# Column lists by one subtraction, searches tied to products, and row constants taken beside the single y blocks

## The chip, the cores and the metric

The kernel runs on one core of one Trainium2 chip. The metric is device time in microseconds (us) of one launch. Before the change the median of three runs was 1048.48 us (1046.01 to 1048.81). The hardware profiler also recorded one execution, and every duration below is from that execution.

Engines: TensorE (PE) multiplies matrices, VectorE (DVE) does elementwise work, reductions and searches, ScalarE (ACT) copies, activations and row sums, GpSimd (POOL) index work and indirect DMA (gathers and scatters), and SyncE (SP) issues plain DMA.

## The reference

Two graph layers over 2708 nodes with 1024 features, each with a residual and a layer norm, all in float32. `adj` is a 0/1 matrix with 10979 ones, some four to a row.

```python
# layer 0, attention masked by adj
q = x @ W_q.T + b_q ; k = x @ W_k.T + b_k ; v = x @ W_v.T + b_v
z = (q @ k.T) / sqrt(1024) * adj
z = where(z == 0, -10000, z)
x = layernorm(x + relu(softmax(z, axis=1) @ v))
# layer 1
x = layernorm(x + adj @ (x @ weight) + bias)
```

## The kernel before

**Sparse form.** The kernel lists the non-zero columns of each row of `adj` and gathers only those rows of `x`. If a list does not fit, or a product of exactly zero makes the mask ambiguous, a flag sends the program to a dense version; with these inputs the sparse one alone runs.

**Lists (`list_columns`, L235 to L252).** `adj` is read in 22 blocks of 128 rows (the last has 20), each cut into six column ranges of growing width, with eight ones stored behind each range. Per range one DVE search (`max_index`, L242) returns the positions of the first eight ones, in order. The ones behind the range stand for "no more". L244 marks the positions that lie inside the range, L247 adds the range's start, L248 sets the others to zero, and three `max` with two `match_replace` keep the 24 largest numbers as the row's `keys`. `count_columns` (L254) sums the row on ACT and then loads a later block of `adj` into the same one of three buffers.

**Families and records.** `sort_begin(f)` and `sort_end(f)` (L657, L678) sort the rows of a family by number of neighbours (family 0: blocks 0 to 7; family 1: blocks 8 to 21). `records_out` scatters one record of 28 words per row (24 columns, then row, degree, offset, one unused word) to DRAM, in sorted order, and reads all back as `tabs`. From then on a block means 128 rows of like degree, with as many gather slots as `SLOTS` says. The 32 longest rows are cut into pieces, the "hub", by `deal_hub`, a generator that is continued by each `next(deal)`.

**Stages, in order of time.**

1. M = W_q^T W_k is formed in 28 half products of four matmuls (`product_of_m`, L757). `EARLY` says how many lists are emitted among them.
2. y = x M for family 0 in four pairs of blocks (`y_pair`), seven half products each, by a scheme that saves one product in eight. Lists, counts and sorting are hung between half products in the table `between`. In a pair, DVE adds one half into another, and the last product needs the bank that such an add has read.
3. y for blocks 8 to 21 one at a time (`y_block`, L386): 16 matmuls each, results copied by ACT. `firsts` holds every fourth matmul.
4. Pair steps: attention sums are turned and multiplied by W_v in ten pairs (`project_pair`), with one step "mean" for the rows that have no neighbours.
5. Layer 1 in the same form, over gathered rows of `x1`, which layer 0 has scattered.

**Attention on DVE.** Beside stages 3 and 4 DVE scores each gathered row against y (L1027, L1143) and sums the rows by their weights (L1086, L1162). A planner hands out these jobs: each step adds the time that DVE is thought to have (`credit`), a job takes its estimated cost from it (1.5 us, and 2.6 us per slot), and jobs that a coming pair needs are forced. A job's first score follows the product before the last.

**Row constants (`row_constants`, L1281).** The test for exact zeros needs x.u per row, u being one vector. In the last three pair steps POOL gathers x for 23 blocks of sorted rows (22 and the hub), 9, 9 and 5 at a time, and DVE multiplies each by u and adds up (L1286). u is spread over the partitions into `u_bc`, which is the tile `part`, once the hub has done with it (L1418). `test_scores` (L1297) uses the sums in layer 1.

**Order.** The program order and the dependencies are the author's; a scheduler orders each engine's instructions ahead of time, by readiness in its own estimate, with program order as priority. On the chip each engine takes its instructions in that order. `follow(later, earlier)` adds a dependency, which moves an instruction behind a matmul in this order. `high_priority` puts the adds of products first among what is ready.

Of the kernel before, what the change touches and what calls it, by code (L numbers as in the profile page):

```python
# [9 lines left out]
F32 = mybir.dt.float32  # L10
BF16 = mybir.dt.bfloat16
I32 = mybir.dt.int32
# [26 lines left out]
KEYS = 24  # L39
RANGES = 6  # L40
CLASSES = list(range(1, 14)) + [15, 17, 20, 24]
EARLY = 13
G1 = 9
RB = 5
REC = 28
ROW, DEG, OFF = 24, 25, 26

# [36 lines left out]
def sparse_part(ctx, tc, x, xT, adj, wqT, wkT, wvT, bq, bk, bv, w1, b1, out):  # L84
# [28 lines left out]
    with es:  # L113
# [12 lines left out]

        def load_rows(dst, src, r0, n, queue=nc.sync):
            m = n // 16 * 16
            queue.dma_start(out=dst[:m], in_=src[r0:r0 + m])
            if m < n:  # L130
                queue.dma_start(out=dst[m:n], in_=src[r0 + m:r0 + n])

# [73 lines left out]

        cuts = [round(N * (i / RANGES) ** 2) for i in range(RANGES + 1)]
        loaded, sorted_, products, applied, began, between = [], [], [], [], [], {}

        AW = N + 8 * RANGES  # L210
        ends = lists.tile([P, RANGES, 8], F32, name="ends")
        base = lists.tile([P, RANGES, 8], F32, name="base")
        for i in range(RANGES):
            nc.vector.memset(ends[:, i], float(cuts[i + 1] - cuts[i]))
            nc.vector.memset(base[:, i], float(cuts[i] + 1))

# [17 lines left out]

        def list_columns():  # L235
            b = listed[0]
            listed[0] += 1
            n, a = rows[b], loaded[b]

            at = lists.tile([P, RANGES, 8], U16, name="at_a", bufs=2)  # L240
            for i in range(RANGES):
                nc.vector.max_index(at[:n, i], ones[:n, :8], a[:n, cuts[i] + 8 * i:cuts[i + 1] + 8 * i + 8])  # L242
            there = lists.tile([P, RANGES, 8], F32, name="there", bufs=2)
            nc.vector.tensor_tensor(there[:n], at[:n], ends[:n], op=ALU.is_lt)  # L244
            few = lists.tile([P, 8 * RANGES], F32, name="few", bufs=2)
            few3 = few.rearrange("p (i k) -> p i k", k=8)
            nc.vector.tensor_tensor(few3[:n], at[:n], base[:n], op=ALU.add)  # L247
            nc.vector.tensor_tensor(few3[:n], few3[:n], there[:n], op=ALU.mult)  # L248
# [132 lines left out]
        def y_store(b, yo):  # L381
            r0, n = b * P, rows[b]
            o0 = r0 - FAMILY * P * (b >= FAMILY)
            nc.sync.dma_start(out=y_ds[b >= FAMILY][o0:o0 + n, :D], in_=yo[:n])

        def y_block(b):  # L386
            yo = yos[b % 3]
            to = halves_of(yo)
            firsts = []
# [12 lines left out]
            load_x()  # L402
            y_store(b, yo)
# [353 lines left out]
        def product_of_m(acc, a, w, start, stop):  # L757
# [477 lines left out]

        STEP, Y_END, Y_LATE, PAIR, EVICT, FLIP, END, SLOT, SMALL = 14.2, 4.8, 1.8, 24.3, 7.5, 2.2, 3.3, 2.6, 1.5
        got, xb_bc, xb_pools, pair_x = {}, [], [], {}
# [38 lines left out]
        nc.vector.memset(c_rows, 0.0)  # L1276
        c_left = list(range(NB + 1))

        u_bc = part

        def row_constants(count):  # L1281
            for k in [c_left.pop(0) for _ in range(count)]:
                n = P if k in (0, NB) else rows[k]
                at = rec_h[:, ROW:ROW + 1] if k == NB else tab0[:, ROW:ROW + 1] if k == 0 else tabs[:n, k, ROW:ROW + 1]
                xg = gather_at(x, at, n, g_tile(), behind=products[-2])
                nc.vector.scalar_tensor_tensor(junkv[:n], xg[:n], 1.0, u_bc[:n], op0=ALU.mult, op1=ALU.mult,  # L1286
                                               accum_out=c_rows[:n, k:k + 1])

# [8 lines left out]
        def test_scores():  # L1297
# [58 lines left out]
        for i, (kind, b) in enumerate(steps):  # L1356
# [29 lines left out]
            if kind == "y":  # L1386
                if FAMILY + 1 <= b < FAMILY + 5:
                    next(deal)
                if 6 <= b - FAMILY < 11:
                    k0 = 3 * (b - FAMILY - 6)  # L1390
                    records_out(*later_records, k0, min(k0 + 3, NB - FAMILY), products[-2])
                if b == FAMILY + 11:
                    records_back(1)
                    nc.sync.dma_start(out=bias_bc, in_=bv.to_broadcast([P, D]))
# [16 lines left out]
            else:  # L1411
# [20 lines left out]
        for p in pending:  # L1432
            p[0](*p[1:])
        assert not jobs and not c_left

# [431 lines left out]
```

## Time and profile before

| | |
|---|---|
| median of three runs | 1048.48 us |
| the profiled execution's own time | 1040.17 us |
| its span, first to last instruction | 1038.3 us |
| mean granted PE clock | 0.977 |
| PE, DVE, POOL, ACT busy | 962.3, 824.4, 564.5, 459.0 us |
| moved by DMA | 229.24 MB, mean 221 GB/s |

Stages by the timeline: M until 132 us, y pairs until 248, single y blocks until 431, pair steps until about 735, layer 1 to the end. A group of instructions is shown by line, engine, operation, tiles, shapes and count; then its busy time and the mean of one, and the idle time ahead of it with what ended that idle time. A line of the waits says which instruction of an engine waited for which of another: us in total, number of times, longest. In the timeline, the square brackets hold the idle time before an instruction.

### The profile page before, as it was taken

To read this page: it belongs to the slowest core of one execution; us is meant where nothing else is said; L and a number is where in the kernel's file an instruction comes from. 1 tells how busy PE (TensorE), PEld (TensorE's weight loads), DVE (VectorE), ACT (ScalarE), POOL (GpSimd) and SP (SyncE) were. 2 spreads that over 40 slices of the span, in tenths; PEclk is the share of its full clock that TensorE was granted. 3 is DMA by queue.
4 is the path that set the end of the run, shared out by engine and by line. 5 is a ranking of instruction groups with operands and counts; after the bars stand their busy time and mean duration, and the time that the engine had idled before them with its cause. 6 is when DMAs were issued, how large, how long until landed. Compare 5 with 4: busy or idle time off the path is not lost.

```text
span 1038.3 us, 10579 instructions
## 1 busy us (share of the span) xinstructions
PE 962.3 (93%) x2723; PEld 453.5 (44%) x2723; DVE 824.4 (79%) x1851; ACT 459.0 (44%) x1142; POOL 564.5 (54%) x455
## 2 busy tenths in 40 slices
PE   7979996899999999999999899997899999988994
PEld 6434443444444444455544444443444444434441
DVE  8999998982768987998999798976569886868532
ACT  4634473554534354224745453334323444361832
POOL 3841045231567656245466576572578888768420
PEclk9989998999999999999999899998999999989998
DMA  9465786666889777257448777698597699987741
GB/s 348 148 189 176 222 275 198 214 203 216 216 249 318 254 216 225 97 145 216 165 124 239 241 222 236 227 282 308 167 308 226 218 297 314 312 249 196 219 109 44
DMA packets 103070, 229.24 MB, mean 221 GB/s; under 512 B 19678, under 2 KB 47078, under 8 KB 103000
## 3 DMA queue, kind: packets, MB, share of 16 engines
q0 software_dynamic: 51152, 159.06, 50.1%
q1 hardware_dynamic: 51848, 69.41, 20.6%
q8 instruction: 23, 0.38, 0.1%
q14 instruction: 47, 0.39, 0.1%
HBM read 218.09 MB, written 33.64 MB: 242 GB/s over the span
## 4 chain that ended last, share of the span: by engine, by line
PE 40%; DVE 25%; DMA 13%; issue 10%; ACT 6%; POOL 5%; SPq 1%; POOLq 0%; DVEq 0%; ACTq 0%
PE po L313 22%; PE po L393 11%; DVE at_a L242 6%; PE tr L393 5%; DMA g<-in_x_dram,tabs 4%; DVE r L1463 2%; DMA xr<-x_d,tabs 2%; ACT junks L989 2%; POOL g L485 2%; DMA g<-x_d,tab 1%; DVE t L335 1%; DVE r L1086 1%; PE tr L942 1%; DMA wq_i<-in_wqT_dram 1%; ACT t L1003 1%
## 5 line engine op out<-in xcount | busy, mean ns | idle before, releaser
L313 PE MATMUL po<-t,s_all 128*128 128x512 f32 x320 | 145.2, 595 | 8.5 <-DVE xr L335 3.1
L485 POOL DMA_INDIRECT g<-in_x_dram,tabs x84 | 111.6, 1329 | 69.5 <-ACT r L1084 14.0
L393 PE MATMUL po<-m,xt 128*128 128x512 f32 x288 | 124.7, 592 | 0.1
L1463 DVE SCALAR_TENSOR_TENSOR r<-g,valid,r 128x1024 f32<-128x1024 f32 x77 | 98.1, 1280 | 16.3 <-issue 6.7
L313 PEld LDWEIGHTS po<-t,s_all 128*128 128x128 f32 x320 | 59.8, 190 | 87.4 <-issue 73.1
L989 ACT ACTIVATE junks<-t,lnm 128x1024 uint8<-128x1024 f32 (+1 forms) x40 | 45.8, 1144 | 115.5 <-DVE lnm L987 115.1
L1027 DVE SCALAR_TENSOR_TENSOR junkv<-yg,g 128x1024 uint8<-128x1024 f32 x69 | 84.3, 1222 | 10.1 <-DMA g<-in_x_dram,tabs 5.5
L485 POOL DMA_INDIRECT g<-x_d,tabs x66 | 77.1, 1168 | 23.2 <-issue 17.6
L1086 DVE SCALAR_TENSOR_TENSOR r<-g,pr,r 128x1024 f32<-128x1024 f32 x64 | 82.0, 1281 | 6.4 <-ACT r L1084 5.8
L393 PEld LDWEIGHTS po<-m,xt 128*128 128x128 f32 x288 | 54.6, 190 | 68.2 <-issue 67.4
L242 DVE FIND_INDEX8 at_a<-ones,a 128x8 uint16<-128x83 f32 (+3 forms) x132 | 82.0, 627 | 0.0
L313 PE MATMUL po<-wv,s_all 128*128 128x512 f32 x160 | 75.1, 611 | 6.8 <-DVE t L335 6.8
L943 ACT COPY rT<-tr 128x512 f32<-128x512 f32 x76 | 41.5, 588 | 84.0 <-PE tr L942 70.2
L313 PE MATMUL po<-w,rT 128*128 128x512 f32 x160 | 73.7, 601 | 4.5 <-DVE t L1500 4.2
L258 ACT ACTIVATE junk<-a 128x2756 uint8<-128x2756 uint32 (+1 forms) x22 | 55.0, 2501 | 49.5 <-issue 31.5
L313 PE MATMUL po<-t,rT 128*128 128x512 f32 x160 | 74.3, 607 | 0.9 <-DVE t L335 0.4
L464 ACT ACTIVATE junka<-xt 128x128 f32<-128x128 f32 x168 | 51.8, 308 | 50.1 <-PE po L313 16.7
L313 PE MATMUL po<-wv,rT 128*128 128x512 f32 x160 | 73.2, 606 | 0.0
L313 PE MATMUL po<-w,s_all 128*128 128x512 f32 x160 | 72.5, 593 | 0.0
L1027 DVE SCALAR_TENSOR_TENSOR junkv<-xr,g 128x1024 uint8<-128x1024 f32 x37 | 45.4, 1226 | 18.9 <-DMA g<-in_x_dram,tabs 11.0
L393 PE MATMUL tr<-m,xt 128*128 128x512 f32 x128 | 55.6, 592 | 0.0
L1473 ACT COPY xr<-bias 128x1024 f32<-128x1024 f32 (+1 forms) x22 | 22.8, 1043 | 68.3 <-DVE t L1500 49.7
(418 smaller groups left out, 1868.4 us busy)
## 6 DMA issues: line engine op xcount, KB each, us to landing
xt<-in_xT_dram SPq DMA_DIRECT2D x21, 512.0 KB
y_d<-yo SPq DMA_DIRECT2D x21, 512.0 KB
a<-in_adj_dram SPq DMA_DIRECT2D x21, 413.5 KB
a<-in_adj_dram SPq DMA_DIRECT2D x21, 338.5 KB
a<-in_adj_dram SPq DMA_DIRECT2D x21, 263.5 KB
wq_i<-in_wqT_dram SPq DMA_DIRECT2D x8, 512.0 KB
wk_i<-in_wkT_dram SPq DMA_DIRECT2D x8, 512.0 KB
wv<-in_wvT_dram SPq DMA_DIRECT2D x16, 256.0 KB
```

Source lines behind the costliest of these rows:

```text
L242: nc.vector.max_index(at[:n, i], ones[:n, :8], a[:n, cuts[i] + 8 * i:cuts[i + 1] + 8 * i + 8])
L258: put = nc.scalar.activation(junk[:n], loaded[b][:n, :AW].bitcast(U32), AF.Sign, accum_out=cnt[:n, b:b + 1])
L313: put = nc.tensor.matmul(acc, a[:, k], w[:, k], start=start and k == 0, stop=stop and k == DC // 2 - 1, skip_group_check=True)
L393: put = nc.tensor.matmul(po, xts[b][:, c, :], m_q[c // 4][h][:, c % 4], start=(c == 0), stop=(c == DC - 1))
L464: put = nc.scalar.activation(junka[:, :xt.shape[2]], xt[:, c, :], AF.Copy, accum_out=xs[:, c, b:b + 1])
L485: nc.gpsimd.indirect_dma_start(out=dst[:n], out_offset=None, in_=src, in_offset=bass.IndirectOffsetOnAxis(ap=at, axis=0), bounds_check=N - ...
L943: nc.scalar.copy(rT[:, g * 4:g * 4 + 4, :], tr)
L989: nc.scalar.activation(junks[:n], t[:n], AF.Square, bias=nm[:n], accum_out=vs[:n])
L1027: put = nc.vector.scalar_tensor_tensor(junkv[:n], yg[:n], scale, xg[:n], op0=ALU.mult, op1=ALU.mult, accum_out=s)
L1086: nc.vector.scalar_tensor_tensor(r[:n], xg[j][:n], pr[:n, j:j + 1], r[:n], op0=ALU.mult, op1=ALU.add)
L1463: put = nc.vector.scalar_tensor_tensor(r[:n], xg[:n], ok[:n, j:j + 1], r[:n], op0=ALU.mult, op1=ALU.add)
L1473: follow(nc.scalar.copy(xr[:n], bias1[:n]), last_norm, same=True)
```

## The change

Five things change together.

- **Lists.** The threshold tile `ends` now holds the range's width plus i/16, and one subtraction, `ends - at`, takes the place of compare, add and multiply. A found column gives a number of at least 1, whose fraction tells the range; a missing one gives less than 1. `max` and `match_replace` work on these numbers, so a row's list comes in another order. `sort_begin` turns them into column numbers with six further DVE operations per family, on 128x192 and 128x336 elements. The cuts follow a formula for that (75 i² + i + 2) and move by up to three columns.
- **Searches tied to products.** The first search of a list now follows a matmul: the half product just made in stage 1, the one it hangs on in stage 2.
- **Other places.** `EARLY` is 12, not 13; the y pairs take 2, 3, 3 and 2 lists, not 3, 3, 3 and 0; `sort_begin(1)` comes after the last y pair, not after the third.
- **Row constants of family 1** come from plain rows of x: beside the single y blocks 9 to 13, three blocks at a time, SP loads 128 rows into `part`, DVE multiplies by u. Load and product each follow a matmul of that y block. The sums go into the unused word of the records.
- **Row constants of family 0 and the hub** are gathered as before, but beside single y blocks 10 to 14 and 16 (2, 2, 2, 1, 1 and 1). `u_bc` has a tile of its own, in the place of `bias_bc`, which is loaded later. The planner takes 3.9 us of credit at five steps. The scores of blocks with one slot come one pair step earlier.

```diff
+END2, END1, END0 = 75, 1, 2
-EARLY = 13
+EARLY = 12
-ROW, DEG, OFF = 24, 25, 26
+ROW, DEG, OFF, CON = 24, 25, 26, 27
...
-        cuts = [round(N * (i / RANGES) ** 2) for i in range(RANGES + 1)]
+        cuts = [0] + [END2 * i * i + END1 * i + END0 for i in range(1, RANGES + 1)]
...
-            nc.vector.memset(ends[:, i], float(cuts[i + 1] - cuts[i]))
-            nc.vector.memset(base[:, i], float(cuts[i] + 1))
+            nc.vector.memset(ends[:, i], cuts[i + 1] - cuts[i] + i / 16)
...
-        def list_columns():
+        def list_columns(behind=None):
...
-                nc.vector.max_index(at[:n, i], ones[:n, :8], a[:n, cuts[i] + 8 * i:cuts[i + 1] + 8 * i + 8])
-            there = lists.tile([P, RANGES, 8], F32, name="there", bufs=2)
-            nc.vector.tensor_tensor(there[:n], at[:n], ends[:n], op=ALU.is_lt)
+                put = nc.vector.max_index(at[:n, i], ones[:n, :8], a[:n, cuts[i] + 8 * i:cuts[i + 1] + 8 * i + 8])
+                if i == 0 and behind is not None:
+                    follow(put, behind)
             few = lists.tile([P, 8 * RANGES], F32, name="few", bufs=2)
-            few3 = few.rearrange("p (i k) -> p i k", k=8)
-            nc.vector.tensor_tensor(few3[:n], at[:n], base[:n], op=ALU.add)
-            nc.vector.tensor_tensor(few3[:n], few3[:n], there[:n], op=ALU.mult)
+            nc.vector.tensor_tensor(few.rearrange("p (i k) -> p i k", k=8)[:n], ends[:n], at[:n], op=ALU.subtract)
...
         def sort_begin(f):
...
+            ks = keys[:, bs, :]
             got = lists.tile([P, nb, KEYS], F32, name=f"got{f}")
-            nc.vector.tensor_scalar(got, keys[:, bs, :], 0.0, None, op0=ALU.is_gt)
+            back = lists.tile([P, nb, KEYS], I32, name=f"back{f}")
+            nc.vector.tensor_copy(back, ks)
+            past_end = lists.tile([P, nb, KEYS], F32, name=f"past_end{f}")
+            nc.vector.tensor_sub(past_end, ks, back)
+            nc.vector.tensor_scalar(got, past_end, 256.0 * END2, 32.0 * END2 + 16.0 * END1, op0=ALU.mult, op1=ALU.add)
+            nc.vector.tensor_mul(past_end, past_end, got)
+            nc.vector.scalar_tensor_tensor(past_end, past_end, END2 + END1 + END0 + 1.0, back, op0=ALU.add, op1=ALU.subtract)
+            nc.vector.tensor_scalar(got, ks, 1.0, None, op0=ALU.is_ge)
+            nc.vector.tensor_mul(ks, past_end, got)
...
             while done < EARLY * worked // (7 * DC // 2):
-                list_columns()
+                list_columns(put)
...
-            for k in range(min(3, NB - done)):
+            for k in range(min((2, 3, 3, 2)[b // 2], NB - done)):
                 if k:
-                    between[first + 2 * k] = [lambda put: list_columns()]
+                    between[first + 2 * k] = [list_columns]
                 else:
-                    list_columns()
+                    list_columns(began[-1])
...
                 records_back(0)
+            if b == 6:
                 sort_begin(1)
...
-        bias_bc = hp.tile([P, D], F32, name="bias_bc", tag="bias")
+        u_bc = hp.tile([P, D], F32, name="u_bc", tag="bias")
...
+        def constants_of(xg, n, to, behind):
+            put = nc.vector.scalar_tensor_tensor(junkv[:n], xg[:n], 1.0, u_bc[:n], op0=ALU.mult, op1=ALU.mult,
+                                                 accum_out=to)
+            if behind is not None:
+                follow(put, behind)
+
+        def plain_constants(firsts):
+            for k in range(3):
+                if c_plain:
+                    b = c_plain.pop(0)
+                    n = rows[b]
+                    load_rows(part, x, b * P, n, behind=firsts[k])
+                    constants_of(part, n, c_nat[:n, b - FAMILY:b - FAMILY + 1], firsts[k + 1])
...
+            nc.vector.tensor_copy(c_rows[:, FAMILY:NB], tabs[:, FAMILY:, CON].bitcast(F32))
...
+                if b == FAMILY + 1:
+                    bcast_rows(u_bc, u_col)
+                if 2 <= b - FAMILY < 7 or b == FAMILY + 8:
+                    row_constants((2, 2, 2, 1, 1, 0, 1)[b - FAMILY - 2])
+                if b == FAMILY + 6:
+                    rec1 = later_records[2]
+                    nc.vector.tensor_copy(rec1[:, :, CON:].bitcast(F32), c_nat.unsqueeze(2))
...
                 (y_last if b == NB - 1 else y_block)(b)
+                if 1 <= b - FAMILY < 6:
+                    plain_constants(y_firsts)
+                    credit -= 3 * DOT
...
-                if i == len(steps) - 4:
-                    bcast_rows(u_bc, u_col)
-                if i >= len(steps) - 3:
-                    row_constants((9, 9, 5)[i - len(steps) + 3])
-                if i == len(steps) - 2:
+                if i == len(steps) - 3:
                     for b_ in single:
                         single_scores(b_)
```

More of the change, by code (lines that the diff above doesn't have):

```diff
@@ L125, in sparse_part, with load_rows @@
         wb = tc.alloc_tile_pool(name="wb", bufs=1)
-        def load_rows(dst, src, r0, n, queue=nc.sync):
+        def load_rows(dst, src, r0, n, queue=nc.sync, behind=None):
             m = n // 16 * 16
-            queue.dma_start(out=dst[:m], in_=src[r0:r0 + m])
+            puts = [queue.dma_start(out=dst[:m], in_=src[r0:r0 + m])]
             if m < n:
-                queue.dma_start(out=dst[m:n], in_=src[r0 + m:r0 + n])
+                puts.append(queue.dma_start(out=dst[m:n], in_=src[r0 + m:r0 + n]))
+            if behind is not None:
+                for put in puts:
+                    follow(put, behind)
         bq_sb = const.tile([P, DC], F32, name="bq_sb")
@@ L205, in sparse_part @@
         nc.vector.memset(keys, 0.0)
-        cuts = [round(N * (i / RANGES) ** 2) for i in range(RANGES + 1)]
+        cuts = [0] + [END2 * i * i + END1 * i + END0 for i in range(1, RANGES + 1)]
+        assert cuts[-1] == N
         loaded, sorted_, products, applied, began, between = [], [], [], [], [], {}
@@ L211, in sparse_part @@
         ends = lists.tile([P, RANGES, 8], F32, name="ends")
-        base = lists.tile([P, RANGES, 8], F32, name="base")
         for i in range(RANGES):
-            nc.vector.memset(ends[:, i], float(cuts[i + 1] - cuts[i]))
-            nc.vector.memset(base[:, i], float(cuts[i] + 1))
+            nc.vector.memset(ends[:, i], cuts[i + 1] - cuts[i] + i / 16)
         a_bufs = [la.tile([P, AW + 4], F32, name=f"a{k}", bufs=1) for k in range(3)]
@@ L384, in y_store @@
             nc.sync.dma_start(out=y_ds[b >= FAMILY][o0:o0 + n, :D], in_=yo[:n])
+        y_firsts = []
         def y_block(b):
@@ L388, in y_block @@
             to = halves_of(yo)
-            firsts = []
+            firsts = y_firsts
+            firsts.clear()
             for h in range(NH):
@@ L1233, in finish_pair @@
                 scatter(x1_d[:, :], b, P, t, "x1")
-        STEP, Y_END, Y_LATE, PAIR, EVICT, FLIP, END, SLOT, SMALL = 14.2, 4.8, 1.8, 24.3, 7.5, 2.2, 3.3, 2.6, 1.5
+        STEP, Y_END, Y_LATE, PAIR, EVICT, FLIP, END, SLOT, SMALL, DOT = 14.2, 4.8, 1.8, 24.3, 7.5, 2.2, 3.3, 2.6, 1.5, 1.3
         got, xb_bc, xb_pools, pair_x = {}, [], [], {}
@@ L1276, in sparse_part @@
         nc.vector.memset(c_rows, 0.0)
-        c_left = list(range(NB + 1))
-        u_bc = part
+        c_nat = xa.tile([P, NB - FAMILY], F32, name="c_nat", bufs=1)
+        nc.vector.memset(c_nat, 0.0)
+        c_plain, c_left = list(range(FAMILY, NB)), list(range(FAMILY)) + [NB]
+        def constants_of(xg, n, to, behind):
+            put = nc.vector.scalar_tensor_tensor(junkv[:n], xg[:n], 1.0, u_bc[:n], op0=ALU.mult, op1=ALU.mult,
+                                                 accum_out=to)
+            if behind is not None:
+                follow(put, behind)
+        def plain_constants(firsts):
[5 more added lines that the diff above has]
+                    constants_of(part, n, c_nat[:n, b - FAMILY:b - FAMILY + 1], firsts[k + 1])
         def row_constants(count):
@@ L1285, in row_constants @@
                 xg = gather_at(x, at, n, g_tile(), behind=products[-2])
-                nc.vector.scalar_tensor_tensor(junkv[:n], xg[:n], 1.0, u_bc[:n], op0=ALU.mult, op1=ALU.mult,
-                                               accum_out=c_rows[:n, k:k + 1])
+                constants_of(xg, n, c_rows[:n, k:k + 1], products[-1])
         def single_scores(b):
@@ L1393, in sparse_part @@
                     records_back(1)
+                    bias_bc = hp.tile([P, D], F32, name="bias_bc", tag="bias")
                     nc.sync.dma_start(out=bias_bc, in_=bv.to_broadcast([P, D]))
                 (y_last if b == NB - 1 else y_block)(b)
+                if 1 <= b - FAMILY < 6:
+                    plain_constants(y_firsts)
+                    credit -= 3 * DOT
                 if 3 <= b - FAMILY < 7:
@@ L1433, in sparse_part @@
             p[0](*p[1:])
-        assert not jobs and not c_left
+        assert not jobs and not c_left and not c_plain
         xb_pool.release()
```

## The prediction

> **What bounds the kernel now.** First the page's busy times, then the engines by stage, to see who limits where.
>
> ```profile
> PE 962.3 (93%) x2723; PEld 453.5 (44%) x2723; DVE 824.4 (79%) x1851; ACT 459.0 (44%) x1142; POOL 564.5 (54%) x455
> ```
>
> ```profile
> 26.00:132.00 106.00, 99.50 (x238) 44.37 (x237) 104.89 (x349) 48.93 (x58) 41.78 (x31) 0.97 0.60 185
> 132.00:248.00 116.00, 101.97 (x248) 45.92 (x247) 94.86 (x348) 60.57 (x168) 43.35 (x39) 0.96 0.70 224
> 248.00:431.00 183.00, 182.92 (x483) 81.21 (x482) 140.04 (x235) 77.86 (x296) 103.97 (x78) 1.00 0.75 225
> 431.00:640.00 209.00, 199.02 (x654) 98.41 (x653) 189.66 (x371) 96.93 (x230) 125.90 (x92) 0.98 0.66 198
> 640.00:735.00 95.00, 86.36 (x219) 38.79 (x217) 73.70 (x149) 39.16 (x93) 45.03 (x39) 0.96 0.76 255
> ```
>
> The columns after start, end and length are PE, weight loads, DVE, ACT and POOL, then clock, DMA share and GB/s. PE is the long engine: the end comes sooner only where PE stands still. In the single y blocks (248 to 431) it never does. While M is formed DVE is busy 104.89 of 106 us. So I ask next what PE waited for, first up to 250 us, then from 400 to 735.
>
> ```profile
> PE po L313 <- DVE at_a L242: 10.7, 1, 10.7
> PE tr L313 <- DVE m L335: 6.5, 1, 6.5
> PE po L313 <- DVE yo L335: 3.3, 2, 2.7
> ...
> PE po L313 <- DVE t L335: 9.3, 5, 5.3
> PE tr L942 <- DVE r L1086: 5.0, 3, 4.1
> PE mm L1180 <- DVE tops L1177: 2.4, 1, 2.4
> PE po L313 <- DVE nms L1056: 1.5, 1, 1.5
> ```
>
> Early, 20.5 us, all for DVE. The timeline of PE shows the three longest places:
>
> ```profile
> 57.23 6.17 PE L313 MATMUL tr<-wk_o,wq_o 128*128 128x512 f32 x8 [6.50 <-DVE m L335]
> ...
> 164.07 5.66 PE L313 MATMUL po<-y_t,xt 128*128 128x512 f32 x8 [10.74 <-DVE at_a L242]
> ...
> 715.78 6.28 PE L313 MATMUL po<-wv,s_all 128*128 128x512 f32 x8 [5.31 <-DVE t L335]
> 721.90 3.60 PE L313 MATMUL po<-t,s_all 128*128 128x512 f32 x8
> ```
>
> Eight matmuls take 3.60 us, but 6.17, 5.66 and 6.28 right after these waits: 7.3 us more. DVE's timeline tells why it was late. At 57 us the add that frees the bank stood behind the searches of three lists (35.8 to 56.5); at 164 us the add started at 163.34, behind searches too. At 715 us the add stood behind row-constant products, and those behind gathers that took up to 11 us in the chain that ended last.
>
> ```profile
> L1286 DVE SCALAR_TENSOR_TENSOR junkv<-g,part 128x1024 uint8<-128x1024 f32 x22 | 26.8, 1217 | 4.4 <-DMA g<-in_x_dram,tabs 4.1
> L248 DVE TENSOR_TENSOR few<-few,there 128x48 f32<-128x48 f32 x21 | 9.4, 447 | 0.2
> L247 DVE TENSOR_TENSOR few<-at_a,base 128x48 f32<-128x48 uint16 x21 | 8.4, 402 | 0.0
> L244 DVE TENSOR_TENSOR there<-at_a,ends 128x48 f32<-128x48 uint16 x21 | 7.3, 347 | 0.2
> ```
>
> **What the Trainium skill says.** "TensorE: Matmul & The Clock Gate", Part 1: PE's clock halves after an idle window of some 3.4 us and returns after as long a busy one. The trace agrees: 2.6, 2.1 and 2.7 us lost behind idle times of 6.50, 10.74 and 5.31 us. "SBUF — State Buffer", Who interferes with whom: a DVE instruction with two SBUF inputs waits while GpSimd reads SBUF. The trace agrees: L244 has a median of 208 ns but up to 1270, at 40 to 58 and 130 to 149 us, where POOL adds. "DMA: Bandwidth & Descriptors", Issuing engines are not separate DMA queues: SP's and POOL's transfers share the 16 engines, so moved loads compete with gathers; no single line here shows it, though the DMA share reached 0.97 in 312 to 338 us.
>
> **The change part by part.**
>
> *Lists.* Two of three small operations go. Records overlap by 0.08 us, so a list loses (347 - 80) + (447 - 80) = 0.63 us of DVE, 22 lists 13.9 us. At least 22 x 2 x 0.13 = 5.7, if the remaining subtraction meets all the POOL waits. I take 0.5 a list, 11 us.
>
> *Decoding.* Six more operations per family. Like forms took 241 to 348 ns on 128x192 and 315 to 485 ns on 128x336 (L661, L702, L703): 6 x 0.30 + 6 x 0.40 - 12 x 0.08 = 3.2 us.
>
> *Fewer lists early.* A list is 6 searches at 3.66 us, then 0.11 for the subtraction and 0.7 for max and replace, 4.5 us. Up to the end of the first y pair 14 are due instead of 16. DVE loses there 2 x (4.5 + 0.5) + 14 x 0.5 - 1.3 = 15.7 us. It was saturated and made PE wait 17.2 us by then.
>
> *Ties.* A search can no longer be put ahead of an add whose product ends first. A tied search holds what is behind it on DVE (adds, keys, sorting, the hub), and PE waits for the adds. M needs 28 x 3.43 = 96 us of PE; DVE now has 12 x 4.5 = 54 for lists, 7.3 for adds, 12.4 for differences, 6.3 for sorting and some 4 for POOL's locks, 84 us. It fits, tightly. Of 20.5 + 4.6 (clock) = 25.1 us I take back 20; the bounds are 10 and 25.
>
> *Last y pair.* Two lists (9 us), the rest of the hub's search (some 9), decoding and sorting (9) and adds (2) want 29 of its 24 us, so the sort ends some 5 us late. It was covered by 19 us of idle DVE in 234 to 260. PE can go to the next y block meanwhile; late next are the records, not due before y block 14. I count 1 us, bounds 0 and 8.
>
> *Constants.* The last three pair steps lose 23 gathers (POOL 1.11 us each) and 23 products (1.22 us each, 28 us of DVE). PE's waits from 640 on are 5.31 + 1.47 + 0.44 + 0.43 + 0.37 = 8.0, with the clock 10.7 us. I take 9; bounds 3 and 11.
>
> What moves lands beside the single y blocks. DVE has 183 - 140 = 43 us idle there. The planner's arithmetic, done by hand with 3.9 us taken at five steps, pushes one piece of block 0 (five scores, five sums, 12.6 us) from y block 20 into the step "mean", where two pieces are then forced. Left are 43 - 28 + 12.6 = 27.6 us. `part` is one buffer: load, product, load. The products follow the loads' matmuls by a quarter block, 13.73 / 4 = 3.43 us. A load of that size landed 5.1 us after its issue (x's at 196.85, used at 202.35), so each holds DVE 1.7 us: 14 x 1.7 = 24 us, just inside. PE asks nothing of DVE there: ACT copies the results.
>
> SP is held too, with x's next block and y's store behind; x has four buffers, three blocks (41 us) ahead. DMA: the hardware queue moved 69.41 MB in 20.6% of the span, 1.6 us per 512 KB, the software queue 1.7. 14 loads and 9 gathers are 38 us more; 25% of 183 is 46 us free. POOL's 9 gathers (10 us) queue ahead of x's gathers; POOL idled 79 of 183 us. The transposes for `u_bc` cost PE 1.04 us either way. `bias_bc` comes after y block 19 has begun and is used at 441 us, so its load is hidden. `records_out` now waits for the constants on POOL, with gathers behind: one y block of slack.
>
> *Pair steps.* 12.6 us more DVE work before pair (0, 7), whose last sum was done at 477 us and turned on PE at 505. DVE idled 19 us in 431 to 640, so most is absorbed. I count 5 us of PE, bounds 0 and 13.
>
> Sum: -20 + 1 - 9 + 5 = -23 us. The span goes from 1038.3 to 1015, the profiled execution's own time from 1040.17 to 1017. The median stood 8.3 us above that, so 1025 (1048.48 - 23).
>
> **The rivals.**
>
> *Given back (1038).* Early waits shrink by 15 only, the pair steps return 12: -15 + 1 - 9 + 12 = -11. For it: DVE saturated at 431 to 572. Against: 27 us between block 0's end and its use.
>
> *Ties bind (1036).* Searches wait for products while DVE has nothing else; half the early gain goes: -10 + 1 - 9 + 6 = -12. For it: 84 of 96 us leaves little to idle. Against: DVE ran behind PE throughout.
>
> *Slower (1064): the single `part` buffer.* If a load lands late and DVE stands for it in order, each of 14 holds DVE not 1.7 but 5.1 us: 71 us, 44 beyond the cover. DVE is saturated at the pair steps, so PE pays it: -20 - 9 + 1 + 44 = +16. It decides from where 14 h - 27.6 exceeds the other 28, h = 4.0 us. For it: gathers took up to 11 us under load. Against: at y blocks 9 to 13 the planner gives few jobs, so a held DVE delays little.
>
> *It doesn't do what it says.* A longer first range could overfill a list and send rows to the flag. Counting the ones of the inputs by the new cuts, 19 rows overfill where 20 did, all among the first 23: they are hub rows. Under 1 in 100.
>
> **How the numbers follow.** Forecast 0.48 (1014 to 1036: -20 becoming -25 or -12, +5 becoming 0 or +8); given back 0.20; ties bind 0.10; slower 0.16; all cancelling within the bound, or unforeseen, 0.06. Telling from no change takes about 0.3%, 1045 to 1052. The first three make faster 0.78; the rest leave 0.05 for same and 0.17 for slower. The range 1009 to 1051 leaves out most of the slower case and little at the bottom. The likeliest's own range is 1014 to 1036.
>
> **What would show it.** Lists right: L244 and L248 gone, some 11 to 17 us of DVE busy with them. Ties right: PE's waits up to the last y pair under 8 us, and M ending at 123 us, not 132. Constants right: no L1286 after 640, no wait over 2 us in the last three steps. Wrong: DVE waiting on DMA into `part` for over 30 us, PE waits in 431 to 640 (by the old clock) above 20 us, or PE waiting for the sort's matmul behind the last y pair.

## The result, and the profile after

The kernel became slower: a median of 1090.39 us (1087.77 to 1094.22) against 1047.24 us of the kernel before on the same chip, a ratio of 1.0423 with an interval of 1.0374 to 1.0473. The profiled execution took 1089.38 us, its span 1087.6 us, 49.3 more than the span before. A ratio, here and below, is taken from the executions that count as fast (within 1.5% of the fastest of the same kernel); one of the four of e5 does not and enters only its median.

Lines have moved: L242, L335, L1027, L1086 and L1286 before are L245, L336, L1041, L1100 and L1296 after. First the page's busy times of the changed kernel.

```profile
PE 969.2 (89%) x2723; PEld 458.4 (42%) x2723; DVE 810.2 (74%) x1816; ACT 464.0 (43%) x1142; POOL 552.6 (51%) x441
```

DVE lost 14.2 us of work, as the lists promised, and its share fell from 79 to 74%. The time did not follow. The stretches by stage of the changed kernel (after start, end and length: PE, weight loads, DVE, ACT, POOL, clock, DMA share, GB/s) show where it went wrong.

```profile
26.00:128.40 102.40, 97.83 (x234) 43.46 (x233) 90.06 (x300) 46.47 (x56) 48.53 (x35) 0.98 0.62 190
128.40:244.70 116.30, 103.57 (x248) 46.49 (x247) 96.48 (x364) 62.70 (x170) 35.55 (x35) 0.96 0.67 211
244.70:442.40 197.70, 185.02 (x490) 82.10 (x488) 120.09 (x223) 69.30 (x264) 91.97 (x70) 0.97 0.76 234
442.40:476.60 34.20, 0.01 (x1) 0.01 (x1) 31.45 (x45) 8.54 (x30) 14.74 (x13) 0.57 0.52 174
...
676.00:780.00 104.00, 103.58 (x266) 47.44 (x265) 65.25 (x137) 48.87 (x116) 32.74 (x26) 1.00 0.56 177
```

M and the y pairs end at 244.7 us, 3.3 sooner. The end of layer 0 (676 to 780) is clean: PE is busy for 103.58 of 104 us. But between 442.4 and 476.6 PE does nothing at all. The timeline of PE names the places, with the three longest waits in brackets.

```profile
187.34 5.62 PE L314 MATMUL po<-y_t,xt 128*128 128x512 f32 x8 [8.25 <-DVE yo L336]
...
403.21 5.15 PE L448 MATMUL po<-m,x_last 128*32 128x256 f32 x64 [12.32 <-ACT yo L334]
...
476.60 0.48 PE L1184 MATMUL tr<-ident,nm 128*128 128x128 f32 x1 [34.56 <-DVE nm L1163]
```

The last line is the hub's first turning, the step that follows the y blocks; it came at 430.90 before. In four pieces, by the spans:

| up to | before | after | difference |
|---|---|---|---|
| end of the y pairs | 248.0 | 244.7 | -3.3 |
| the hub's first turning | +182.9 | +231.9 | +49.0 |
| layer 1's first turning (742.65 and 784.90) | +311.75 | +308.3 | -3.4 |
| the end | +295.65 | +302.7 | +7.0 |

The whole loss lies beside the single y blocks. There DVE's own waits tell it, first of the kernel before (248 to 430.9), then of the changed one (244.7 to 476.6).

```profile
DVE junkv L1027 <- DMA g<-in_x_dram,tabs: 11.0, 7, 2.3
DVE alike L616 <- PE tr L615: 9.9, 1, 9.9
DVE junkv L1027 <- PE tr L393: 7.4, 1, 7.4
DVE r L1086 <- ACT r L1084: 5.8, 4, 1.6
```

```profile
DVE junkv L1296 <- DMA part<-in_x_dram: 40.7, 11, 6.4
DVE junkv L1041 <- DMA g<-in_x_dram,tabs: 19.4, 6, 6.5
DVE alike L620 <- PE tr L619: 9.9, 1, 9.9
```

The two stretches as a whole, before and after (columns as above):

```profile
248.00:430.90 182.90, 182.82 (x482) 81.11 (x481) 139.94 (x235) 77.75 (x296) 103.97 (x78) 1.00 0.75 225
...
244.70:476.60 231.90, 185.02 (x491) 82.11 (x489) 151.55 (x267) 77.84 (x293) 106.71 (x83) 0.91 0.72 226
```

So 49.0 us of length are 11.6 us more work of DVE and 37.4 us more idle time, and 40.7 us of idle time are one wait, for the loads into `part`. DVE's timeline shows the round:

```profile
322.36 1.23 DVE L1296 SCALAR_TENSOR_TENSOR junkv<-part,u_bc 128x1024 uint8<-128x1024 f32 x1 [2.79 <-DMA part<-in_x_dram]
...
327.71 1.23 DVE L1296 SCALAR_TENSOR_TENSOR junkv<-part,u_bc 128x1024 uint8<-128x1024 f32 x1 [4.11 <-DMA part<-in_x_dram]
```

One product of 1.23 us, and the next 5.35 us later; the rest is standing: a load starts when the product before has freed `part`, and DVE stands for it. From 312 to 352 us DVE was busy for 13.3 of 40 us, all of it row constants. The scores of the next piece came at 352.28, behind the last of these.

How did that reach PE, whose results ACT copies? By ACT's queue:

```profile
361.31 0.30 ACT L1079 ACTIVATE pr<-scores,nms 128x6 f32<-128x6 f32 x1 [21.41 <-DVE nms L1070]
...
381.99 0.30 ACT L1079 ACTIVATE pr<-scores,nm 128x4 f32<-128x4 f32 x1 [12.96 <-DVE nm L1070]
...
393.28 1.05 ACT L484 COPY yg<-y_bc 128x1024 f32<-128x1024 f32 x1 [8.85 <-DVE junkv L1041]
...
402.59 0.57 ACT L334 COPY yo<-po 128x512 f32<-128x512 f32 x1
```

The softmax's exponential (L1079) waits for DVE's maximum, a copy into a tile of gathered y (L484) for DVE's last reading of that tile, and the copies of y stand behind both. At 390.9 PE had no free bank until the copy at 402.59: 12.3 us. The rest of DVE's lag came due at the hub: PE waited 34.6 us, and DVE was busy for 31.45 of the 34.2 us from 442.4 to 476.6.

### The profile page after: what moved, and what is told of

It reads as the page before. It is cut to its first block, busy times and chain, and to the rows that moved or that the text cites. A ratio compares the mean times of both kernels' runs of the same rounds, so it can differ in the third digit from the quotient of the medians.

```text
span 1087.6 us, 10470 instructions
## 1 busy us (share of the span) xinstructions
PE 969.2 (89%) x2723; PEld 458.4 (42%) x2723; DVE 810.2 (74%) x1816; ACT 464.0 (43%) x1142; POOL 552.6 (51%) x441
## 3 DMA queue, kind: packets, MB, share of 16 engines
q0 software_dynamic: 49232, 152.14, 45.9%
## 4 chain that ended last, share of the span: by engine, by line
PE 44%; DVE 19%; DMA 12%; issue 12%; POOL 8%; ACT 3%; SPq 0%; POOLq 0%; DVEq 0%; ACTq 0%
PE po L314 27%; PE po L397 8%; PE tr L397 4%; PE tr L314 3%; POOL g L489 3%; DMA xr<-x_d,tabs 3%; DVE r L1100 2%; DVE junkv L1041 2%; DMA g<-x_d,tabs 2%; DVE at_a L245 2%; POOL tab_d L724 2%; DVE t L336 1%; DVE r L1498 1%; POOL wk_i L304 1%; DMA g<-x_d,tab 1%
## 5 line engine op out<-in xcount | busy, mean ns | idle before, releaser
L489 POOL DMA_INDIRECT g<-in_x_dram,tabs x84 | 115.7, 1378 | 90.9 <-DVE got L670 28.7
L1041 DVE SCALAR_TENSOR_TENSOR junkv<-yg,g 128x1024 uint8<-128x1024 f32 x84 | 102.3, 1218 | 31.8 <-DMA g<-in_x_dram,tabs 20.5
L1498 DVE SCALAR_TENSOR_TENSOR r<-g,valid,r 128x1024 f32<-128x1024 f32 x77 | 97.9, 1280 | 11.6 <-DMA g<-x_d,tabs 9.0
L1100 DVE SCALAR_TENSOR_TENSOR r<-g,pr,r 128x1024 f32<-128x1024 f32 x64 | 81.8, 1280 | 3.4 <-ACT r L1098 2.9
L245 DVE FIND_INDEX8 at_a<-ones,a 128x8 uint16<-128x234 f32 (+5 forms) x132 | 82.2, 627 | 0.0
L314 PE MATMUL po<-wv,s_all 128*128 128x512 f32 x160 | 72.5, 593 | 3.0 <-DVE s_all L1215 1.6
L943 POOL DMA_INDIRECT x_d<-t,tabs x22 | 27.1, 1233 | 65.0 <-ACT rstd L1014 25.9
L473 POOL DMA_INDIRECT xr<-in_x_dram,tabs x22 | 26.9, 1221 | 53.9 <-DVE scores L1050 33.3
## 6 DMA issues: line engine op xcount, KB each, us to landing
wk_i<-in_wkT_dram SPq DMA_DIRECT2D x8, 512.0 KB, 10.9
```

Source lines behind the costliest of these rows:

```text
L245: put = nc.vector.max_index(at[:n, i], ones[:n, :8], a[:n, cuts[i] + 8 * i:cuts[i + 1] + 8 * i + 8])
L314: put = nc.tensor.matmul(acc, a[:, k], w[:, k], start=start and k == 0, stop=stop and k == DC // 2 - 1, skip_group_check=True)
L489: nc.gpsimd.indirect_dma_start(out=dst[:n], out_offset=None, in_=src, in_offset=bass.IndirectOffsetOnAxis(ap=at, axis=0), bounds_check=N - ...
L943: put = nc.gpsimd.indirect_dma_start(out=dst, out_offset=bass.IndirectOffsetOnAxis(ap=tabs[:n, b, ROW:ROW + 1], axis=0), in_=src[:n], in_o ...
L1041: put = nc.vector.scalar_tensor_tensor(junkv[:n], yg[:n], scale, xg[:n], op0=ALU.mult, op1=ALU.mult, accum_out=s)
L1100: nc.vector.scalar_tensor_tensor(r[:n], xg[j][:n], pr[:n, j:j + 1], r[:n], op0=ALU.mult, op1=ALU.add)
```

## The experiments

All ratios are to the kernel before, run in turn with each; the medians take in more executions, so a ratio is not always the quotient of the two. The runs were on four chips (e1 to e4; e5 to e8; e9 to e11; e12), so runs of different groups are compared by their ratios.

| | kernel | median, us | before, us | ratio | interval |
|---|---|---|---|---|---|
| e1 | lists, ties and places | 1039.51 | 1043.64 | 0.9963 | 0.9933 to 0.9994 |
| e2 | constants alone | 1094.55 | 1043.64 | 1.0508 | 1.0438 to 1.0579 |
| e3 | whole change, no plain loads | 1042.41 | 1043.64 | 0.9994 | 0.9973 to 1.0015 |
| e4 | whole change, nine buffers | 1060.43 | 1043.64 | 1.0166 | 1.0097 to 1.0235 |
| e5 | e1, degrees read later | 1035.53 | 1043.89 | 0.9841 | 0.9766 to 0.9915 |
| e6 | e1 untied | 1030.69 | 1043.89 | 0.9853 | 0.9786 to 0.9921 |
| e7 | e3 without the credit | 1072.36 | 1043.89 | 1.0249 | 1.0184 to 1.0313 |
| e8 | e5, nine constants moved | 1041.67 | 1043.89 | 0.9979 | 0.9960 to 0.9998 |
| e9 | e5 untied | 1033.58 | 1045.50 | 0.9882 | 0.9847 to 0.9917 |
| e10 | e8 untied, softmax tied | 1042.77 | 1045.50 | 0.9982 | 0.9965 to 0.9998 |
| e11 | e9, softmax tied | 1032.32 | 1045.50 | 0.9862 | 0.9823 to 0.9902 |
| e12 | one subtraction alone | 1033.18 | 1043.70 | 0.9890 | 0.9855 to 0.9926 |

**Which half, and what of it (e1 to e4).** e1 is the changed kernel with the row constants put back:

```diff
-                if 1 <= b - FAMILY < 6:
-                    plain_constants(y_firsts)
-                    credit -= 3 * DOT
...
+                if i >= len(steps) - 3:
+                    row_constants((9, 9, 5)[i - len(steps) + 3])
```

> Lists, ties and their places as in the changed kernel; row constants as before (all 23 gathered in the last three pair steps). Theory A (the loss comes from VectorE standing on the plain loads of x) and theory B (it comes from the work moved beside the single y blocks) both give the early part alone: the y pairs ended 3.3 us sooner in the changed kernel, so 1044, at most 2 us away. Theory C (lists that arrive late or in another order slow the sort, the records and the attention behind them) gives over 1060, with PE waits in the pair steps that look like those of the changed kernel.

e2 is the other half on the kernel before (EARLY 13, `list_columns` as before, with `plain_constants`).

> The kernel before with the new row constants alone: plain rows of x beside single y blocks 9 to 13, gathers beside 10 to 14 and 16, credit of 3.9 us at five steps; lists and their places as before. Theories A and B: the whole loss, 1047 + 46 = about 1093, with DVE waits on the loads into part of some 40 us and one PE wait of over 25 us behind the last y block. Theory C: under 1060.

e3 takes the loads out of the changed kernel and leaves the products in place; they multiply u by itself, so the constants of family 1 are left out:

```diff
-                    load_rows(part, x, b * P, n, behind=firsts[k])
-                    constants_of(part, n, c_nat[:n, b - FAMILY:b - FAMILY + 1], firsts[k + 1])
+                    constants_of(u_bc, n, c_nat[:n, b - FAMILY:b - FAMILY + 1], firsts[k + 1])
```

> The changed kernel without the 14 plain loads of x: the 14 products stay in their places, tied to the same matmuls, but multiply u by itself, so the constants of family 1 are not computed. Theory A: the 40.7 us of DVE waits on the loads go, and with them PE's 12.3 and 34.6 us; 1090 - 47 = 1043, perhaps 5 less as the later stalls go too. Theory B (the moved products and the pushed piece are too much work): at most the 11 us of PE's wait for the copies, so over 1075.

e4 keeps the loads and gives each another buffer:

```diff
-                    load_rows(part, x, b * P, n, behind=firsts[k])
-                    constants_of(part, n, c_nat[:n, b - FAMILY:b - FAMILY + 1], firsts[k + 1])
+                    xg = g_tile()
+                    load_rows(xg, x, b * P, n, behind=firsts[k])
+                    constants_of(xg, n, c_nat[:n, b - FAMILY:b - FAMILY + 1], firsts[k + 1])
```

> The changed kernel with the plain rows loaded into the nine rotating buffers of the gathers instead of the one tile part; loads and products keep their ties, a quarter block apart. Theory A with the single buffer as the cause: a load no longer waits for the product before, so a hold is at most a landing of 4.0 to 5.1 less 3.43, under 1.7 us each, 24 us in all instead of 41; DVE's lag falls by 17 us or more and the PE wait of 34.6 us by as much: 1065 to 1073. If the tie of a product a quarter block behind its load were the cause, it stays over 1080. Theory B: over 1080 as well, but with no DVE wait on the loads.

Theory A stands, rivals B and C fall; only e4 came out 5 us below the range that was expected of it. The constants alone cost 5.1% and carry the same wait at the hub (35.7 us), with 32.5 us of DVE waits on the loads; the lists alone cost nothing (0.996). Without the loads, with every product still in its place, the whole 4.2% goes, and PE's wait at the hub falls from 34.6 to 1.9 us. With nine buffers 2.6 of the 4.2% come back. DVE's waits of e4 from 245 us on:

```profile
DVE junkv L1296 <- DMA g<-in_x_dram,tabs: 12.3, 3, 6.3
DVE junkv L1296 <- DMA g<-in_x_dram: 11.5, 4, 5.7
```

The second line is what is left of the 40.7 us. The first is new: DVE now stands for three of the gathered constants. Why those came late was not tried. PE's wait at the hub was 14.5 us. One rival is left open in the remaining 1.7%: the loads are also traffic beside the gathers. DVE's waits for gathered rows at the scores (L1041) were 19.4 us in the changed kernel, against 11.0 before. In e4, with the same loads, they were 6.4, which speaks against it; but no run moves the same bytes with no product behind them.

**What remained without the loads (e7, e8, e10).** e3 was no faster than before, though its end of layer 0 was as clean. I blamed the piece of block 0 that the planner's charge pushes behind the y blocks, and took the charge out:

```diff
-        STEP, ..., SMALL, DOT = 14.2, 4.8, 1.8, 24.3, 7.5, 2.2, 3.3, 2.6, 1.5, 1.3
+        STEP, ..., SMALL, DOT = 14.2, 4.8, 1.8, 24.3, 7.5, 2.2, 3.3, 2.6, 1.5, 0.0
```

> The changed kernel without the 14 plain loads (the products multiply u by itself, so family 1's constants are not computed) and with no credit taken by the planner for them. Without the loads alone it took as long as before although the early part and the end of layer 0 had gained some 12 us. Theory P (the piece of block 0 that the planner pushed from the y blocks into the step of the mean makes the new waits of 16 us between 430 and 630 us): 8 to 12 us less than without the loads, about 1032. Theory W (the 28 us of products on VectorE make it late wherever the pieces are placed): within 4 us of 1042.

A miss, and in the other direction: by the ratios some 27 us slower than e3. Two of PE's waits in e7:

```profile
PE tr L956 <- DVE tops L1186: 13.8, 1, 13.8
...
PE po L448 <- ACT yo L334: 9.1, 1, 9.1
```

With the piece back beside the y blocks, DVE is late for the hub even with no load to stand for. The charge was not the harm; it was what kept DVE's lag from being larger. Theory P falls, and theory W falls with it in its number. That a piece of 12.6 us is worth 27 us is more than either theory had, and why was not tried. With the piece pushed, the products did find some room, as e3's stretch of the y blocks shows:

```profile
244.70:431.40 186.70, 184.84 (x498) 82.88 (x496) 153.22 (x272) 79.50 (x293) 114.50 (x83) 1.00 0.78 243
```

Against the kernel before that is 13.3 us more work of DVE, 9.5 us less idle time and 3.8 us more length. e8 asks for room with the smallest part: only the nine gathered constants are moved, without loads or charge.

```diff
+                if 2 <= b - FAMILY < 7 or b == FAMILY + 8:
+                    row_constants((2, 2, 2, 1, 1, 0, 1)[b - FAMILY - 2], u_early, products[-1])
...
-                    row_constants((9, 9, 5)[i - len(steps) + 3])
+                    row_constants((5, 5, 4)[i - len(steps) + 3])
```

> The lists alone with the tie of e5, and of the row constants only the nine gathered ones of family 0 and the hub beside the single y blocks (2, 2, 2, 1, 1 and 1, as in the changed kernel, products tied), no plain loads, no credit taken; the 14 of family 1 are gathered in the last three pair steps, 5, 5 and 4. Theory A: gathers of nine rotating buffers hold VectorE little, nine products (11 us) fit into its idle 43 us there, and the last steps have 14 gathers instead of 23, so PE's wait of 5.1 us there shrinks by half: some 5 us less than e5, about 1027. If any moved constant costs what it saves, the same as e5.

Another miss: a ratio of 0.998, not something below e5's 0.984. Eleven microseconds of work that should have vanished in 43 idle ones brought PE's wait for ACT back, and DVE got a new wait, of four of the moved products for their gathers:

```profile
PE po L445 <- ACT yo L334: 12.4, 1, 12.4
...
DVE junkv L1297 <- DMA g<-in_x_dram,tabs: 11.4, 4, 7.6
```

From the end of the y pairs to the hub's sum of weights e8 took 203.0 us and e5 187.5; DVE worked 9.2 us more and was idle 6.3 us more. So the run does not show what work alone would have cost: the products brought waits of their own.

e10 asks whether ACT's order or DVE's lag is the cause. The exponential follows the last product emitted (the searches are untied, for which see below).

```diff
-                nc.scalar.activation(pr[:n, :m], z, AF.Exp, bias=nm, accum_out=den[:n])
+                put = nc.scalar.activation(pr[:n, :m], z, AF.Exp, bias=nm, accum_out=den[:n])
+                if left_y:
+                    follow(put, products[-1])
```

> e8 (nine gathered constants beside the y blocks) with untied searches, and the softmax's exponential on ScalarE tied to the last product emitted before it while y blocks are left, so that it stands behind more of the copies of y in ScalarE's order. Theory Q (PE's wait of 12.4 us in e8 comes from those copies standing behind an exponential that waits for VectorE): that wait falls under 3 us, the y blocks end 10 us or more sooner than they would, and the time is below e9's, about 1022. If VectorE's lag comes back to PE in another way, at the hub's transposes or the first pairs, the wait moves there and the time stays near e8 less 9 for the ties, about 1031 or above.

> e9 with the same tie of the exponential, constants all in the last three pair steps: the control for e10. No wait of PE for a copy of y is in e6, so theory Q expects no change from e9; if the tie delays the sums that follow the exponentials, 2 to 6 us more.

The wait at the copy fell from 12.4 to 1.98 us, as theory Q said, and the time did not follow. PE's waits and timeline of e10:

```profile
PE tr L953 <- DVE tops L1187: 12.0, 1, 12.0
```

```profile
385.11 3.66 PE L445 MATMUL po<-m,x_last 128*32 128x256 f32 x64 [1.98 <-ACT yo L334]
```

The 12 us moved to the hub. ACT's queue is one of two ways by which DVE's lag reaches PE; the lag itself is the cause. e11, the control without moved constants, is as fast as e9 within the intervals. Between e11 and e10 the nine moved constants cost 0.012, some 12 us, as much as their 11 us of work. That is no test of work alone either: up to the hub's sum of weights e10 is 19.0 us longer than e11, with 10.9 us more work and 8.1 us more idle time of DVE, 7.4 us of waits for the moved gathers among it; the pair steps, with nine products fewer, give part of it back.

**Why the early gain was 3.3 us (e5, e6, e9, e12).** DVE's timeline in the changed kernel has two waits that were shorter or not there before:

```profile
45.85 3.39 DVE L788 TENSOR_TENSOR m_t<-wk_o,wk_o 128x2048 f32<-128x2048 f32 x1 [4.99 <-ACT junk L305]
...
173.49 0.15 DVE L589 CAST deg_r<-rec_r 128x1 f32<-128x1 int32 x1 [14.41 <-DMA rec_r<-tab_d,r_i]
```

Before, the first had none and the second was 4.43 us at 178.51. L589 reads the hub's degrees from the records, which only then come back from DRAM. Up to the end of the first y pair PE was 11.2 us ahead of the kernel before (158.5 us, not 169.7); 7.4 of these were lost again in the second pair, in which DVE stood there and PE then waited 8.25 us. e5 ties that operation, in e1's kernel, behind a later product:

```diff
-            nc.vector.tensor_copy(deg_r, rec[:, DEG:DEG + 1])
+            follow(nc.vector.tensor_copy(deg_r, rec[:, DEG:DEG + 1]), products[-1])
```

> The kernel of the lists alone (constants as before), with one tie more: the hub's small operation that reads the records' degrees (L586 there) follows the last product emitted before it, so VectorE reaches it long after the records are back. Theory S (the VectorE time that the lists gave up is spent standing there, 13.8 us in the lists alone against 4.4 before, and the adds behind it are late): PE's wait of 7.7 us in the second y pair and some 2 us of clock go, so 0.992 to 0.994 of the lists alone, about 8 us less. If the two lists behind that operation are the cause, not the standing, the wait stays and so does the time.

e6 takes the ties of the searches out of e1 instead, and e9 does both:

```diff
-                list_columns(put)
+                list_columns()
```

> The kernel of the lists alone, searches tied to no product; one subtraction, EARLY 12 and the places 2, 3, 3, 2 are kept. If the ties bind (VectorE stands at a tied search with nothing else to do): 3 us or more faster than the lists alone, and the y pairs end sooner. If the ties are what lets the adds go first: PE's waits at 153 us and in M grow again, by 3 to 8 us, and it is that much slower. If neither: the same within 0.3%, and the gain is of the fewer operations and the places.

> e6 (lists by one subtraction, no ties of the searches, constants as before) with the tie of e5 (the operation that reads the degrees follows the last product emitted before it). If the standing at the records still costs PE something there: below e6, about 1027. In e6 VectorE stood there 7.2 us and PE had no wait in the second y pair, so the theory that it is free once untied searches fill the time before gives the same as e6, a ratio of 0.985 to the kernel before.

Each gains over e1: e5 0.012, e6 0.011. The intervals of e1 and of each of the two do not overlap, but e5 rests on three executions from 1027.5 to 1039.6 us, the slowest of which is the profiled one; e6's four all lie below the fastest of e1. In e5 PE's wait in the second y pair fell from 7.7 to 1.8 us. In e6 DVE stood for 1.6 us, not 5.0, at M's difference: ACT was done at about the same time (45.9 us), but untied searches ran before it, and M ended at 125.2 us instead of 128.2. At the records it stood 7.2 us, not 13.8; it came there as early (159.4 us), and the records were back at 166.6 instead of 173.0. Of these 6.4 us, 3.5 are their scatters, which landed 2.4 instead of 5.9 us after the last was issued, 1.2 are an earlier issue, and the rest is the reading back. Why they landed faster was not tried. Both edits together (e9) give no more than one. So with the lists alone the ties bound, and with the standing operation moved (e5 against e9) they cost nothing that these few executions can tell.

e12 is the kernel before with the subtraction and the decoding alone.

> The kernel before with the lists by one subtraction and their decoding alone: EARLY 13, places 3, 3, 3 and 0, untied, constants as before. By the forecast's sums VectorE gives up 16 lists x 0.5 - 1.3 = 6.7 us up to the first y pair (of the 15.7 that it gives up with the two lists moved as well). If that goes to PE one for one while VectorE is saturated: 0.994, about 6 us less than before; with the places moved (e6) 0.985. If the freed time is spent standing at the records' degrees (4.4 us in the kernel before) or for ScalarE ahead of M's difference: the same as before, and the whole gain of e6 is that of the places.

It gives 0.989, a larger gain than the 0.994 of its sum, which lies outside the interval; why was not tried. The intervals of e6 and e9 cover it: the new places add nothing that these runs can tell. e12, e6 and e9, all with the constants where they were, are 1.1 to 1.5% faster than the kernel before.

## Why the prediction was wrong

The forecast was 1025 us within 1009 to 1051. The slower rival was told with its mechanism, at 1064, and given 0.16.

*Lists and decoding: right.* Groups of the changed kernel:

```profile
L1296 DVE SCALAR_TENSOR_TENSOR junkv<-part,u_bc 128x1024 uint8<-128x1024 f32 (+1 forms) x14 | 17.1, 1224 | 40.7 <-DMA part<-in_x_dram 40.7
...
L1296 DVE SCALAR_TENSOR_TENSOR junkv<-g,u_bc 128x1024 uint8<-128x1024 f32 x9 | 11.0, 1221 | 0.2
...
L249 DVE TENSOR_TENSOR few<-ends,at_a 128x48 f32<-128x48 f32 (+1 forms) x22 | 8.5, 385 | 0.0
```

Three operations of 25.1 us became one of 8.5; less 44 overlaps of 0.08 that is 13.1 us, inside 5.7 to 13.9. The six decoding operations took 4.8 us in sum, 3.8 with their overlaps taken off, for 3.2.

*Early part, -20: wrong, -3.3.* DVE was freed of the work: up to the end of M alone it was busy for 111.6 us, not 125.8. The step that failed is "I take back 20", which let the freed time of DVE serve PE and had no term for what DVE would stand at next. DVE stood 5.0 us for ACT in M and then 14.4 - 4.4 = 10.0 us more for the records in the second y pair, about as much as the 15.7 us that were to be freed. M ended at 128.4, not 123, and PE's waits up to the last y pair were 17.3 us, not under 8. The rival "ties bind" was the right one for this part, with e5's addition.

*Last y pair, +1: right.* PE waited 1.11 us there.

*End of layer 0 and pair steps, -9 + 5: right.* The piece from the hub to layer 1 is 3.4 us shorter. No L1296 is left there, and new waits of PE of 3.07 and 4.05 us (at 558 and 641) take part of it back. That they come from the pushed piece fits the runs: e2, e3 and e4, which push it, have both, and e7, which does not, has neither. What the forecast did not see is that the piece left in its place would have cost far more (e7).

*Constants beside the y blocks, 0: wrong, +49.0.* Three terms of "43 - 28 + 12.6 = 27.6" and "14 x 1.7 = 24 us, just inside" failed.

- "43 us idle": this was the largest. It was counted as room for any work and any hold. Before, the four lines above alone are 34.1 of the 43.0 us: DVE stood for gathers, for PE and for ACT. In the changed kernel DVE's idle time without the loads' waits was still 80.4 - 40.7 = 39.7 us, so 3.3 of the 43 served as cover. That is not zero for all work: in e3, where the products have no loads to wait for and the piece is pushed, 9.5 us of 13.3 vanished. But in e7, e8 and e10, where the moved products stand for gathers or the piece stays, DVE's idle time up to the hub's sum of weights grew instead (by 6.7, 6.3 and 8.1 us against before, e5 and e11).
- "each holds DVE 1.7 us": it was 40.7 / 14 = 2.9 on average, 3.7 where DVE waited. The landing was shorter than I took (a median of 4.0 us, not 5.1). But in the rounds shown it counts from the freeing of `part`, not from the matmul a quarter block ahead, wherever DVE is late for the product before; then the quarter block is lost.
- "PE asks nothing of DVE there": by ACT's queue it does, and at the hub.

With a cover of zero the forecast's own sum would have turned: 24 us of holds and 28 of products, less the 12.6 pushed, are 39 us, against 28 gained. The slower rival named the place, the buffer and the wait that was seen, and its sign for failure (over 30 us of DVE waits into `part`) is what came. That its 44 us beside the y blocks are near the measured 49.0 is luck: it had 71 us of holds where 40.7 came, and 27.6 us of cover where 3.3 us of the 43 served. It fell short in sum by early gains that were not there. The argument against it, that a held DVE delays little where the planner gives few jobs, overlooked that the next job stands behind the held products.

*Left open.* Layer 1 took 7.0 us more, where nothing was changed but the read of the constants. Up to the start of PE's last product that is 3.8 us. PE's waits in layer 1 are the same (16.0 and 16.2 us before), and by the granted clocks of three stretches of the same lengths (65, 100 and 90 us; 0.97, 1.00 and 0.94, and before 1.00, 1.00 and 0.96) an estimate is 7.4 us lost to the clock, 3.6 before. Why the clock was lower was not tried. The other 3.2 us lie behind PE's work, between the last store's issue and the end, and stay open.

## What to carry to other kernels

The sum of an engine's idle time is not yet cover. New work fills an idle stretch only if it stands ahead of the instruction that waits there, so ask first what ends each stretch, and price also what the new work will itself wait for: that wait holds everything behind it. Here 3.3 us of 43 served where the new work brought waits, and 9.5 us of 13.3 of work vanished where it brought hardly any (2.2 us, in e3). A load into a single buffer whose consumer is on a busy engine costs that engine a landing per round, once it is late, even if the load is tied to an earlier step (here 40.7 us in 14 rounds). When an engine is freed of work, look for the next thing that it will stand at, and move that instruction first.

## What was not expected of the hardware

A DVE addition of 128x1 elements took 3.39 us in e1 (at 173.38 us; the same line took 0.15 before). In that time POOL ran four additions and subtractions of 128x512 from 173.01 to 178.10, and DVE's ended as the third of them did, at 176.7. "SBUF — State Buffer", Who interferes with whom, in the Trainium skill says that the port pair shared with GpSimd is an exclusive lock. The trace agrees, and shows that the wait can last beyond the POOL instruction that was running, here to the end of the third that follow each other. In e5, where the addition came at 240 us, it took 0.15 us.

After PE's idle 34.56 us the first turning took 0.48 us instead of 0.27, and the granted clock of 442.4 to 476.6 us was 0.57. In the Trainium skill "TensorE: Matmul & The Clock Gate", Part 1, says that PE's clock halves after an idle window; the trace agrees with that too.
